# SAGE sums of a four-layer graph stack: h stored as three bf16 pieces

## The chip, the cores and the metric

The kernel runs on one core of a Trainium2 chip. The metric is device time in microseconds, from the first to the last instruction of the core. Before the change three runs gave 2575.82, 2585.0 and 2585.8 us; their median is 2585.0.

## The reference

There are 3327 nodes with 512 features (padded to 3328 rows, 26 blocks of 128) and a sparse 0/1 adjacency matrix. Four layers follow each other, each in the form x = x + layer(relu(layernorm(x))). Layers 0, 2 and 3 are graph attention with 8 heads. Layer 1, which the change is about, is GraphSAGE:

```python
mask = (adj > 0).astype(x.dtype)
deg = jnp.sum(mask, axis=1, keepdims=True)
agg = mask @ x / jnp.maximum(deg, 1.0)          # x here is h = relu(layernorm(x1))
self_f = x @ W_self + b_self
nb_f = agg @ W_nb + b_nb
out = jnp.concatenate([self_f, nb_f], axis=-1) @ W_comb + b_comb
return jax.nn.relu(out)
```

All of it is in float32.

## The kernel before, in words

**Neighbours by lists.** The rows of the output are taken in 52 groups of 64. For each group a first stage makes a list of the nodes that are a neighbour of any row in it, in chunks of 128. `CAPS` holds the number of chunks of each group: 22 for the first, down to 4 for the last, 359 in all. `mask` holds, for each chunk, a 128 x 64 matrix of 0 and 1 in one byte each. A chunk's 128 rows are fetched from a table in device memory by an indirect DMA that POOL issues (`gather`, L1115).

**Layer 0** ends with its output in `y`, 26 blocks of 128 x 512 float32 in on-chip memory. What comes next is the part that the change touches:

- Batch norm statistics: DVE, ACT and PE form the variance (L1352 to L1361).
- The norm stage. `normed(c)` works on two blocks. DVE applies batch norm and the residual (L1370 to L1372), the result goes to `x1`, DVE takes layer norm statistics (L1377), ACT makes h in place in `y` (L1385), and SP stores both blocks to `h_dram`, 512 float32 a row (L1386). `own(c)` then transposes a block of h, multiplies by the folded weights of the self half (PE, `s_ps`, L1396) and adds a bias into `y` (DVE, L1397). In program order `own` of a pair comes after `normed` of the next pair; all `normed` have their inputs at once, so DVE can run ahead of PE.
- SAGE. A block of 128 output rows is two groups, u = 0 and 1. `parts` cuts their chunks into units of up to `SUNIT` = 2 chunks. `load(i)` copies the masks of a unit to float32 on ACT (`z_mask`, L1453) and gathers up to two chunks of h (`z_rows`); `SROWS` = 8 units of buffers rotate, and the loads run `SAHEAD` = 2 parts ahead. Then PE adds mask.T @ rows into `sage_acc` (L1472): group u has the 64 output partitions from u * 64, so the two groups use different column halves of the array. Before each pair of chunks `tick()` moves on the work that follows: `ending` scales the finished sum by the degree, transposes it, multiplies by the folded neighbour weights (`n_ps`, L1421), adds and stores `x2`, and `proj` (an instance of `Following`) makes layer 2's table row by row (`p_ps` L795, `p_sd` L803, `p_wh` L816, `p_tr` L824).

No gather can start before the whole of `h_dram` is stored, since a list can name any row.

**Order and memory.** In the attention layers the order on PE, DVE and ACT is written out by hand. In the norm stage and SAGE it is not: the compiler orders ready instructions by program order and by its own estimate of times. Pools of on-chip memory are laid on each other as a stack. `proj = following(...)` at L1344 takes the memory of layer 2's projection, and starts its weight load `fWt` (1 MB, L749), before the batch norm stage.

Of the kernel before, what the change touches and what calls it, by code (L numbers as in the profile page):

```python
# [23 lines left out]
F32 = mybir.dt.float32  # L24
BF16 = mybir.dt.bfloat16
# [7 lines left out]
ALU = mybir.AluOpType  # L33
# [5 lines left out]
P = 128  # L39
H = 8  # L40
F = 64
D = H * F
# [8 lines left out]
GB = 64  # L51
CAPS = (22, 15, 13, 12, 11, 10, 9, 9, 9) + 4 * (8,) + 6 * (7,) + 11 * (6,) + 21 * (5,) + (4,)
# [5 lines left out]
UNIT = 3  # L58
SUNIT = 2
SROWS = 8  # L60
SAHEAD = 2
SMALL = 53.0
SHIFT = 20.0
# [638 lines left out]
def rsqrt(nc, pool, cs, v, scale=1.0, bufs=3):  # L702


    n = v.shape[1]
    y = pool.tile([P, n], F32, name="rs_y", tag=f"rs_y{n}", bufs=bufs)
    g = pool.tile([P, n], F32, name="rs_g", tag=f"rs_g{n}", bufs=bufs)
    nc.scalar.activation(g, v, AF.Ln, scale=scale, bias=cs["eps"])
    nc.scalar.activation(y, g, AF.Exp, scale=-0.5)

    def step():
        h = pool.tile([P, n], F32, name="rs_h", tag=f"rs_h{n}", bufs=bufs)
        nc.vector.tensor_scalar(h, v, -0.5 * scale, -0.5 * EPS, ALU.mult, ALU.add)
        if n == 1:
            nc.vector.tensor_scalar(g, y, y, h, ALU.mult, ALU.mult)
        else:
            nc.vector.tensor_tensor(g, y, y, ALU.mult)
            nc.vector.tensor_tensor(g, g, h, ALU.mult)
        nc.vector.scalar_tensor_tensor(y, g, 1.5, y, ALU.add, ALU.mult)
        return y  # L720

    return step
# [364 lines left out]
def sparse(ctx: ExitStack, tc: tile.TileContext, t: dict, out: bass.AP, WA, ls, cs, idx, rdeg, first):  # L1087
# [5 lines left out]
    nc = tc.nc  # L1093
    N = out.shape[0]
    NP = t["x"].shape[0]
    NB = NP // P
    NCH = ls.n
    PG = P // GB

    def used(c):  # L1100
        return min(P, N - c * P)

    dram = ctx.enter_context(tc.tile_pool(name="fdram", bufs=1, space=DRAM))
# [10 lines left out]
    def gather(dst, src, k):  # L1114
        nc.gpsimd.indirect_dma_start(  # L1115
            out=dst, out_offset=None, in_=src[:, :], in_offset=bass.IndirectOffsetOnAxis(ap=idx[:, k : k + 1], axis=0)
        )


    def attend(layer, table, r_dram, finish, tick=lambda: None, home=None):  # L1120
# [11 lines left out]
        with tc.tile_pool(name=f"fatt{layer}", bufs=2) as ap, tc.tile_pool(  # L1132
# [57 lines left out]
            def load(i):  # L1190
# [8 lines left out]
                if layer == 0:  # L1199
# [8 lines left out]
                    nc.scalar.activation(mask[:, k0 : k0 + n, :], on[:, :n].rearrange("p k w b -> p k (w b)"), AF.Sign)  # L1208

            load(0)  # L1210
            for i, (g, k0, n, begins, stops) in enumerate(units):
                gt = rows.pop(i)
# [9 lines left out]
                wt = ap.tile([P, UNIT, H, GB], F32, name="wgt", tag="wgt", bufs=3)  # L1222
                nc.vector.tensor_tensor(wt[:, :n], mx[:, :n], mk.unsqueeze(2).to_broadcast(full), ALU.mult)  # L1223
                load(i + 1)
                later()
                if begins:
# [22 lines left out]
    def following(lx, layer, wl, W, pb=1):  # L1249

        table = dram.tile([NP, ROW], I32, name=f"table{layer}")
        r_dram = dram.tile([ls.G, 2, H, GB], F32, name=f"r_dram{layer}")
        pp = lx.enter_context(tc.tile_pool(name=f"fproj{layer}", bufs=1))
        pps = lx.enter_context(tc.tile_pool(name=f"fproj_ps{layer}", bufs=1, space=PSUM))
        return Following(tc, cs, N, wl, W, WA, table, r_dram, pp, pps, pb)
# [20 lines left out]


    wx_dram = dram.tile([2, KC, P, D], F32, name="wx_dram")
    h_dram = dram.tile([NP, D], F32, name="h_dram")
    with ExitStack() as mx:  # L1280
        mid = mx.enter_context(tc.tile_pool(name="fmid", bufs=1))

# [58 lines left out]
        Wx = mid.tile([P, 2, KC, D], F32, name="fWx")  # L1341
        nc.sync.dma_start(Wx, wx_dram.rearrange("k kc p o -> p k kc o"))

        proj = following(mx, 2, 1, t["L2_gnn_W"], 2)  # L1344
        gp = mx.enter_context(tc.tile_pool(name="fsage", bufs=2))
        gps = mx.enter_context(tc.tile_pool(name="fsage_ps", bufs=2, space=PSUM))
        two = [P, 2, D]
        with tc.tile_pool(name="fbn", bufs=1) as bp:
            var_ps = gps.tile([P, D], F32, name="var_ps", tag="n_ps")
            for c in range(0, NB, 2):  # L1350
# [3 lines left out]
                for i in range(2):  # L1354
                    k = used(c + i)
# [7 lines left out]
        with tc.tile_pool(name="fln", bufs=1) as bp:  # L1363


            def normed(c):
                xr = bp.tile(two, F32, name="bn_x", tag="bn_x", bufs=3)
                nc.sync.dma_start(xr, t["x"][c * P : (c + 2) * P, :].rearrange("(k p) o -> p k o", p=P))
                yy = y[:, c : c + 2, :]
                nc.vector.tensor_tensor(yy, yy, gam.unsqueeze(1).to_broadcast(two), ALU.mult)  # L1370
                nc.vector.tensor_tensor(yy, yy, bet.unsqueeze(1).to_broadcast(two), ALU.add)
                nc.vector.scalar_tensor_tensor(xr, yy, 0.0, xr, ALU.max, ALU.add)  # L1372
                nc.sync.dma_start(x1[c * P : (c + 2) * P, :].rearrange("(k p) o -> p k o", p=P), xr)
                mv = bp.tile([P, 2, nc.vector.BN_AGGR_DIM], F32, name="ln_mv", tag="ln_mv", bufs=3)
                for i in range(2):
                    st = bp.tile([P, nc.vector.BN_STATS_DIM], F32, name="ln_st", tag="ln_st", bufs=3)
                    nc.vector.bn_stats(st, xr[:, i, :])  # L1377
                    nc.vector.bn_aggr(mv[:, i, :], st)
                r = rsqrt(nc, bp, cs, mv[:, :, 1:2].rearrange("p k o -> p (k o)"))()
                if c + 2 == NB:  # L1380
                    nc.vector.tensor_tensor(r[:, 1:2], r[:, 1:2], cs["real"], ALU.mult)
                ng = bp.tile([P, 2, 1], F32, name="ln_ng", tag="ln_ng", bufs=3)
                nc.vector.scalar_tensor_tensor(ng, mv[:, :, 0:1], -1.0, r.unsqueeze(2), ALU.mult, ALU.mult)
                for i in range(2):
                    nc.scalar.activation(yy[:, i, :], xr[:, i, :], AF.Relu, scale=r[:, i : i + 1], bias=ng[:, i, :])  # L1385
                nc.sync.dma_start(h_dram[c * P : (c + 2) * P, :].rearrange("(k p) o -> p k o", p=P), yy)  # L1386

            def own(c):
                tp = gps.tile([P, KC, P], F32, name="h_ps", tag="a_ps")
                for kc in range(KC):  # L1390
                    nc.tensor.transpose(tp[:, kc, :], y[:, c, kc * P : (kc + 1) * P], cs["ident"])
                hT = bp.tile([P, KC, P], F32, name="hT", tag="hT", bufs=2)
                nc.scalar.copy(hT, tp)  # L1393
                ps = gps.tile([P, D], F32, name="s_ps", tag="n_ps")
                for kc in range(KC):
                    nc.tensor.matmul(ps, hT[:, kc, :], Wx[:, 0, kc, :], start=(kc == 0), stop=(kc == KC - 1))  # L1396
                nc.vector.tensor_tensor(y[:, c, :], ps, bias, ALU.add)  # L1397

            for c in range(0, NB, 2):
                normed(c)  # L1400
                for i in range(2):
                    if c:
                        own(c - 2 + i)
            for i in range(2):
                own(NB - 2 + i)

        ends = []

        def ending(b, acc):
# [21 lines left out]
        def tick():  # L1431
            for e in list(ends):
                if next(e, 0) == 0:
                    ends.remove(e)
            proj.tick()
# [6 lines left out]
        loaded = {}  # L1442

        def load(i):
            if i >= len(parts):
                return
            zs = loaded[i] = []
            for u, kn in enumerate(parts[i][1]):
                if kn is not None:
                    k0, n = kn  # L1450
                    zt = gp.tile([P, SUNIT, D], F32, name="z_rows", tag="z_rows", bufs=SROWS)
                    mf = gp.tile([P, SUNIT, GB], F32, name="z_mask", tag="z_mask", bufs=SROWS)
                    nc.scalar.copy(mf[:, :n, :], mask[:, k0 : k0 + n, :])  # L1453
                    for k in range(n):
                        gather(zt[:, k, :], h_dram, k0 + k)
                        zs.append((k, u, k0 + k, mf[:, k, :], zt[:, k, :]))
            zs.sort(key=lambda x: x[:2])

        for i in range(SAHEAD):
            load(i)  # L1460
        for i, (b, _, begins, stops) in enumerate(parts):
            load(i + SAHEAD)
            if begins:
                acc = gps.tile([P, D], F32, name="sage_acc", tag="sage_acc")
            at = -1
            for r, u, k, m, z in loaded.pop(i):
                if r != at:
                    at = r
                    tick()
                g = b * PG + u  # L1470
                f, l = k == ls.first[g], k == ls.first[g] + CAPS[g] - 1
                nc.tensor.matmul(acc[u * GB : (u + 1) * GB, :], m, z, start=f, stop=l)  # L1472
            if stops:
                ends.append(ending(b, acc))
        while ends:
# [4 lines left out]
    with ExitStack() as l3:  # L1480
        at2 = proj
        proj = following(l3, 3, 2, t["L3_gnn_W"])
# [90 lines left out]
```

## Time and profile before

The profiled execution took 2951.92 us, with a span of 2950.1 us; the runs without the profiler have a median of 2585.0 us. All times of single instructions below are of the profiled execution.

| what | profiled execution |
|---|---|
| span | 2950.1 us, mean granted TensorE clock 0.791 |
| PE, DVE, ACT, POOL busy | 73%, 60%, 38%, 47% of the span |
| norm stage, first h_dram store to last | 954.7 to 1020.7 us |
| SAGE, first gather to last | 1024.6 to 1610.6 us |
| software DMA queue (all gathers) | 404.86 MB, 47.2% of 16 engines' span |
| all HBM reads and writes | 498.74 MB and 59.68 MB |

In a row of the profile, `z_rows<-h_dram,idx` means that the instruction writes `z_rows` and reads `h_dram` and `idx`; then come the number of instructions, the sum of their time and the mean of one in ns, and the idle time of the engine just before them with what ended it. PEld is PE's loading of weights, which can run beside a matmul. A busy share tells how full an engine is, not whether it sets the pace.

### The profile page before, as it was taken

The page shows a single profiled execution, that of the slowest core. Times are in us where ns is not written, and L with a number is a line of the kernel's source. Part 1 is how long each engine was busy: PE and PEld are TensorE (multiplying, and loading weights), DVE is VectorE, ACT ScalarE, POOL GpSimd, SP SyncE. Part 2 cuts the span into 40 slices and gives each one's busy share as a digit, 9 for nine tenths or more (in the row PEclk, how much of TensorE's full clock was granted, in tenths as well). Part 3 has the DMA queues.
Part 4 walks back from the last instruction along what each step waited for, and adds up shares of the span by engine and source line. Part 5 has one row for each costly group of instructions (what it writes and reads, how often), then busy time and mean ns, then how long its engine had stood idle before and what let it go on. Part 6 is the DMA issues. An engine that isn't in the chain of part 4 may idle for free.

```text
span 2950.1 us, 54237 instructions
## 1 busy us (share of the span) xinstructions
PE 2161.4 (73%) x21320; PEld 1372.2 (47%) x21320; DVE 1781.5 (60%) x2194; ACT 1115.7 (38%) x4044; POOL 1381.8 (47%) x1482
## 2 busy tenths in 40 slices
PE   4777577767775976888998567877777657767775
PEld 2444354555552422233333355655555345556564
DVE  7648587878786800011111377777776277888886
ACT  4543022333434412344455213555666501232333
POOL 1001365666550055665554365555444066666563
PEclk9778688977777997899999777777787766675765
DMA  7761577877662746666665466666565166667774
GB/s 309 282 251 46 174 235 233 252 214 209 201 203 82 246 145 187 189 207 212 198 196 183 133 184 186 200 198 188 178 178 166 45 192 190 193 200 198 201 205 131
DMA packets 188773, 562.09 MB, mean 191 GB/s; under 512 B 37732, under 2 KB 42272, under 8 KB 185182
## 3 DMA queue, kind: packets, MB, share of 16 engines
q0 software_dynamic: 115456, 404.86, 47.2%
q1 hardware_dynamic: 73054, 153.67, 14.7%
q8 instruction: 171, 2.80, 0.4%
q14 instruction: 92, 0.75, 0.1%
HBM read 498.74 MB, written 59.68 MB: 189 GB/s over the span
## 4 chain that ended last, share of the span: by engine, by line
PE 54%; issue 16%; ACT 9%; another core or an unknown queue 3%; DVE 3%; DMA 2%; POOL 1%; SPq 0%; DVEq 0%; ACTq 0%; POOLq 0%
PE facc L1237 28%; PE p_wh L816 7%; PE sage_acc L1472 5%; PE n_ps L1421 3%; PE r_bc L1148 2%; PE p_sd L803 2%; PE s_ps L1396 2%; ACT v_row L820 2%; ACT fhp L1175 1%; PE fwx_ps L1314 1%; PE bmean_ps L1324 1%; PE p_ps L795 1%; ACT hT L798 1%; DMA rows<-table,idx 1%
## 5 line engine op out<-in xcount | busy, mean ns | idle before, releaser
L1115 POOL DMA_INDIRECT rows<-table,idx x1077 | 1023.4, 950 | 873.2 <-PE facc L1237 361.7
L1237 PE MATMUL facc<-rows,wgt 128*64 128x65 f32 x17232 | 975.3, 268 | 412.7 <-issue 394.5
L1237 PEld LDWEIGHTS facc<-rows,wgt 128*64 128x64 f32 x17232 | 826.5, 176 | 628.7 <-issue 576.9
L1223 DVE TENSOR_TENSOR wgt<-mx,mask 128x1536 f32<-128x1536 f32 (+1 forms) x405 | 638.4, 1576 | 158.6 <-PE facc L1237 75.0
L1216 DVE TENSOR_TENSOR mx<-r_bc,rows 128x1536 f32<-128x1536 f32 (+1 forms) x405 | 639.6, 1579 | 144.7 <-PE facc L1237 65.9
L1115 POOL DMA_INDIRECT z_rows<-h_dram,idx x359 | 339.4, 945 | 387.0 <-ACT hT L1393 139.5
L1175 ACT ACTIVATE fhp<-sums,rd 64x64 f32<-64x64 f32 x832 | 219.8, 334 | 137.0 <-DVE rd L1169 71.8
L1472 PE MATMUL sage_acc<-z_rows,z_mask 128*64 128x512 f32 x718 | 225.2, 639 | 9.5 <-DMA z_rows<-h_dram,idx 6.2
L816 PE MATMUL p_wh<-fWt,hT 128*128 128x512 f32 x416 | 227.7, 695 | 1.4 <-ACT s_col L810 1.4
L1165 ACT COPY sums<-facc 128x260 f32<-128x260 f32 x156 | 57.7, 370 | 405.0 <-PE facc L1237 354.3
L813 DVE TENSOR_SCALAR s_col<-s_col 128x8 f32<-128x8 f32 x52 | 9.2, 177 | 306.0 <-issue 135.9
L1208 ACT ACTIVATE mask<-on 128x192 uint8<-128x192 uint16 (+1 forms) x135 | 46.5, 344 | 378.8 <-DVE on L1202 214.1
L816 PEld LDWEIGHTS p_wh<-fWt,hT 128*128 128x128 f32 x416 | 90.3, 228 | 109.8 <-issue 105.3
L820 ACT ACTIVATE v_row<-p_wh,v_row 128x64 f32<-128x64 f32 x416 | 90.4, 328 | 125.8 <-PE p_wh L816 99.3
L1426 DVE TENSOR_TENSOR s_o<-n_ps,bn_y 128x512 f32<-128x512 f32 x26 | 18.0, 691 | 192.2 <-issue 95.6
L1036 POOL DMA_DIRECT2D list_b<-shift x12 | 5.9, 503 | 273.4 <-DVE shift L990 273.4
L680 PE MATMUL wh_ps<-fWt,hT 128*128 128x512 f32 x208 | 128.9, 777 | 0.0
L803 PE MATMUL p_sd<-WA,hT 128*128 128x16 f32 x416 | 74.4, 303 | 70.3 <-ACT hT L798 46.2
L803 PEld LDWEIGHTS p_sd<-WA,hT 128*128 128x128 f32 x416 | 71.8, 246 | 103.9 <-ACT hT L798 59.6
L1175 ACT ACTIVATE bn_y<-sums,rd 64x64 f32<-64x64 f32 x416 | 109.5, 333 | 2.4 <-DVE rd L1169 0.5
L1421 PE MATMUL n_ps<-fWx,aT 128*128 128x512 f32 x208 | 106.1, 646 | 5.6 <-ACT aT L1417 5.5
L1148 PE MATMUL r_bc<-r_two,fones 2*128 2x512 f32 x156 | 95.3, 615 | 14.8 <-issue 8.1
(198 smaller groups left out, 2108.0 us busy)
## 6 DMA issues: line engine op xcount, KB each, us to landing
adj_i<-in_adj SPq DMA_DIRECT2D x26, 1664.0 KB
table<-v_row SPq DMA_DIRECT2D x78, 264.0 KB
rows<-table,idx POOLq DMA_INDIRECT x1077
fin_x<-fx SPq DMA_DIRECT2D x52, 256.0 KB
ln_x<-in_x SPq DMA_DIRECT2D x26, 256.0 KB
bn_x<-in_x SPq DMA_DIRECT2D x13, 512.0 KB
fx<-bn_x SPq DMA_DIRECT2D x13, 512.0 KB
fsage_x<-fx SPq DMA_DIRECT2D x26, 256.0 KB
```

The costliest lines, as they stand in the source:

```text
L680: nc.tensor.matmul(wh, hT[:, kc, :], self.Wt[:, kc, :], start=(kc == 0), stop=(kc == KC - 1))
L803: nc.tensor.matmul(sd[:, : 2 * H], hT[:, kc, :], WA[wl][:, kc, :], start=(kc == 0), stop=(kc == KC - 1))
L816: nc.tensor.matmul(wh, hT[:, kc, :], self.Wt[:, kc, :], start=(kc == 0), stop=(kc == KC - 1))
L820: nc.scalar.mul(V[:, h, 0:F], wh[:, h * F : (h + 1) * F], V[:, h, F : F + 1])
L1115: nc.gpsimd.indirect_dma_start(out=dst, out_offset=None, in_=src[:, :], in_offset=bass.IndirectOffsetOnAxis(ap=idx[:, k : k + 1], axis=0))
L1148: nc.tensor.matmul(rb, ones[0:2, :].bitcast(F32R), rrs.pop(g).bitcast(F32R), start=True, stop=True)
L1175: nc.scalar.mul(hp[o0 : o0 + GB, h * F : (h + 1) * F], sm[mine, q, 0:F], rd[mine, q, :])
L1216: nc.vector.tensor_tensor(mx[:, :n], rbs[g].unsqueeze(1).to_broadcast(full), gt[:, :n, H * (F + 1) : ROW].unsqueeze(3).to_broadcast(full), ...
L1223: nc.vector.tensor_tensor(wt[:, :n], mx[:, :n], mk.unsqueeze(2).to_broadcast(full), ALU.mult)
L1237: nc.tensor.matmul(accs[g][v * GB : (v + 1) * GB, q * (F + 1) : (q + 1) * (F + 1)], wt[:, k, h, :], gt[:, k, h * (F + 1) : (h + 1) * (F + 1)],
L1421: nc.tensor.matmul(ps, aT[:, kc, :], Wx[:, 1, kc, :], start=(kc == 0), stop=(kc == KC - 1))
L1472: nc.tensor.matmul(acc[u * GB : (u + 1) * GB, :], m, z, start=f, stop=l)
```

## The change

h is made as before, and then split into three bf16 numbers whose sum is h: the upper 16 bits of the float32 number (read in place, as every second 16-bit word), the upper 16 bits of what is left, and the rest. `h_dram` holds the three pieces side by side, 1536 bf16 numbers a row (3072 bytes in place of 2048). The mask is copied to bf16, and a chunk's sum is three matmuls with bf16 operands, one for each piece, all added into the same float32 accumulator. Within a part the loop now goes over chunk pairs, then pieces, then the two groups. The memory of the next layer's projection is allotted after the norm stage rather than before it, and its weight load moves with it.

```diff
+PIECES = 3
...
-    h_dram = dram.tile([NP, D], F32, name="h_dram")
+    h_dram = dram.tile([NP, PIECES * D], BF16, name="h_dram")
...
-        proj = following(mx, 2, 1, t["L2_gnn_W"], 2)
         gp = mx.enter_context(tc.tile_pool(name="fsage", bufs=2))
...
-                nc.sync.dma_start(h_dram[c * P : (c + 2) * P, :].rearrange("(k p) o -> p k o", p=P), yy)
+                for i in range(2):
+                    hi = yy[:, i, :].bitcast(BF16)[:, 1::2]
+                    hp = bp.tile([P, PIECES, D], BF16, name="h_pieces", tag="h_pieces", bufs=2)
+                    rest = bp.tile([P, D], F32, name="h_rest", tag="h_rest", bufs=2)
+                    nc.vector.tensor_tensor(rest, yy[:, i, :], hi, ALU.subtract)
+                    nc.scalar.copy(hp[:, 0, :], hi)
+                    hi = rest.bitcast(BF16)[:, 1::2]
+                    nc.vector.tensor_tensor(hp[:, 2, :], rest, hi, ALU.subtract)
+                    nc.scalar.copy(hp[:, 1, :], hi)
+                    b = c + i
+                    nc.sync.dma_start(h_dram[b * P : (b + 1) * P, :], hp.rearrange("p t o -> p (t o)"))
...
+        proj = following(mx, 2, 1, t["L2_gnn_W"], 2)
         ends = []
...
-                    zt = gp.tile([P, SUNIT, D], F32, name="z_rows", tag="z_rows", bufs=SROWS)
-                    mf = gp.tile([P, SUNIT, GB], F32, name="z_mask", tag="z_mask", bufs=SROWS)
+                    zt = gp.tile([P, SUNIT, PIECES * D], BF16, name="z_rows", tag="z_rows", bufs=SROWS)
+                    mf = gp.tile([P, SUNIT, GB], BF16, name="z_mask", tag="z_mask", bufs=SROWS)
...
-            at = -1
-            for r, u, k, m, z in loaded.pop(i):
-                if r != at:
-                    at = r
+            zs = loaded.pop(i)
+            for r in range(SUNIT):
+                now = [z for z in zs if z[0] == r]
+                if now:
                     tick()
-                g = b * PG + u
-                f, l = k == ls.first[g], k == ls.first[g] + CAPS[g] - 1
-                nc.tensor.matmul(acc[u * GB : (u + 1) * GB, :], m, z, start=f, stop=l)
+                for j in range(PIECES):
+                    for _, u, k, m, z in now:
+                        g = b * PG + u
+                        f = k == ls.first[g] and j == 0
+                        l = k == ls.first[g] + CAPS[g] - 1 and j == PIECES - 1
+                        nc.tensor.matmul(acc[u * GB : (u + 1) * GB, :], m, z[:, j * D : (j + 1) * D], start=f, stop=l)
```

## The prediction

> **What bounds the kernel now.** I read the page first for the costs and shapes, then windows of busy time to find what the change can reach, then the chain of waits and POOL's order of time inside them. The diff touches two neighbouring stages: the norm stage (942 to about 1020 us of the span, where h is made and stored) and SAGE (first gather at 1024.6, last PE sum at 1632 us). Elsewhere no instruction changes. From the windows of busy time (length, then busy us of PE, PEld, DVE, ACT and POOL with counts, granted clock, DMA share, GB/s):
>
> ```profile
> 942.00:1020.00 78.00, 63.21 (x186) 31.33 (x187) 76.17 (x173) 32.93 (x68) 0.00 (x0) 0.90 0.74 259
> 1046.00:1075.00 29.00, 27.91 (x80) 12.28 (x81) 4.15 (x6) 4.35 (x10) 5.66 (x7) 0.94 0.19 58
> 1075.00:1111.00 36.00, 19.91 (x60) 4.66 (x56) 0.00 (x0) 4.08 (x15) 27.41 (x29) 0.92 0.68 199
> 1300.00:1632.00 332.00, 297.74 (x994) 119.57 (x990) 41.34 (x128) 165.74 (x703) 180.15 (x191) 0.95 0.62 194
> ```
>
> The norm stage is DVE's: 76 of 78 us. From 1046 to 1075 PE is full (own halves of the rows) and the gathers stand. From 1075 to 1111 the gathers lead: 29 in 36 us, PE half idle. From 1300 on PE is 90% busy. So inside SAGE two limits alternate, POOL's stream of gathers and PE, and neither has much room. POOL's order of time shows both its pace and its stops:
>
> ```profile
> 1024.60 0.94 POOL L1115 DMA_INDIRECT z_rows<-h_dram,idx  x1 [139.47 <-ACT hT L1393]
> 1043.35 0.94 POOL L1115 DMA_INDIRECT z_rows<-h_dram,idx  x1 [0.30 <-issue]
> ...
> 1057.98 0.94 POOL L1115 DMA_INDIRECT z_rows<-h_dram,idx  x1 [8.30 <-PE sage_acc L1472]
> ...
> 1066.97 0.94 POOL L1115 DMA_INDIRECT z_rows<-h_dram,idx  x1 [6.79 <-PE sage_acc L1472]
> ...
> 1075.00 0.94 POOL L1115 DMA_INDIRECT z_rows<-h_dram,idx  x1 [5.84 <-PE sage_acc L1472]
> 1076.25 0.94 POOL L1115 DMA_INDIRECT z_rows<-h_dram,idx  x1 [0.30 <-issue]
> ```
>
> One gather each 1.25 us when nothing stops it (16 from 1024.60 to 1043.35), then stops while PE works off its own rows. All 359 cost 449 us at that pace; from 1024.6 to the last at 1610.6 it is 586, so POOL stands for 137 us. The waits of that stretch say for whom:
>
> ```profile
> POOL z_rows L1115 <- PE sage_acc L1472: 92.8, 34, 8.3
> POOL z_rows L1115 <- PE p_tr L824: 46.4, 10, 7.3
> POOL z_rows L1115 <- remote: 12.4, 4, 4.4
> ```
>
> The PE waits are slots that PE's sums have not freed. The sums themselves, from the page:
>
> ```profile
> L1472 PE MATMUL sage_acc<-z_rows,z_mask 128*64 128x512 f32 x718 | 225.2, 639 | 9.5 <-DMA z_rows<-h_dram,idx 6.2
> L1115 POOL DMA_INDIRECT z_rows<-h_dram,idx x359 | 339.4, 945 | 387.0 <-ACT hT L1393 139.5
> ```
>
> Two records for a chunk. In order of time 34 of them run from 1073.65 in 7.94 us, the two halves of 64 columns at once: (7.94 - 0.59 of the last one's length) / 17 = 0.43 us for a record, 0.86 for a step of one or two chunks. The chain of waits puts 12% of 1020 to 1660 us on "another core or an unknown queue"; such pieces are stalls of ACT. The longest starts in the first burst of gathers:
>
> ```profile
> 1032.79 13.59 another core or an unknown queue
> ```
>
> **What the Trainium skill says.** "FP8 and Floating Point Precision", TensorE Precision Notes: true fp32 takes four passes through the array. The trace agrees if each of the two records holds two passes; then a pass over 512 columns is 0.43/2 = 0.214 us. "TensorE: Matmul & The Clock Gate", Back-to-back issue gap, gives 216 ns for a bf16 matmul of 512 columns; no row here shows one, so 0.214 is an estimate from the records that this page supports. "VectorE: DVE Perf Modes", perf-mode tier table: tensor_tensor with fp32 operands has no faster mode; the trace's 128x512 fp32 bn_stats and sums at 0.60 us from start to start agree. "Runtime: NRT & Kernel Launch", Instruction fetch mechanics: instructions come by DMA in 16 KiB blocks, "mostly hidden". The page's instruction queue (171 packets, 2.80 MB) fits the size; the ACT stalls end when the gathers run dry (ACT resumes at 1046.45, DMA share 0.74 before 1046 and 0.11 after), so hidden is not what I see, if they are fetches at all.
>
> **The change, part by part.**
>
> The split, 26 blocks: two DVE subtractions and two ACT copies each. DVE: 52 x 0.60 us = 31 us (bounds 28, were a bf16 result somewhat quicker, and 36 at the full 0.69 us of such a row). DVE has 2 us of idle in this stage, so the norms end 31 us later; while they last, DVE also serves some 7 more of the additions after own (L1397) at 0.60 us, 4 to 5 us. ACT: 52 x 0.59 us (hT copy, 128x512) = 31 us onto 33 of the stage, hidden beside DVE. Two waits are new: DVE's first subtraction waits for ACT's relu, with the next pair's norm queued behind it on DVE (other pairs' work can stand before it, since all norms are ready), and the pieces, in two buffers, wait for the store of two blocks ago, some 3 us against 9 us for two blocks. The store grows from 6.8 to 10.2 MB, in 26 issues of 0.36 us rather than 13; DMA share 0.74 over 78 us becomes about 0.6 over 114, hidden. The last store, issued at 1020.7, moves to about 1057 and the first gather from 1024.6 to about 1061: +36.
>
> What that costs: PE needed until 1073.7 for own. With DVE at about 9 us a pair of blocks against PE's 8.25 (the spacing of 965.94, 974.19, 982.43), own still ends near 1065 to 1072. The stops of POOL at 1044 to 1075 (8.30 + 6.79 + 5.84 + 3.20 = 24 us) were lost time and go. So by 1075 the stream is behind by 36 - 24 = 12 us. Were own also pushed out, it is up to 20; were PE's stops longer than counted, 5.
>
> The sums: a step goes from four passes, 0.86 us, to three, 0.64: 0.21 saved. The caps in pairs make 186 steps; 55 of them lie in the first four blocks, which hold 101 of the gathers and run at the gathers' pace (1075 to about 1175), so nothing is won there. The other 131 give 28 us of PE. Weights are now loaded three times for a chunk rather than twice, 64 columns at 0.14 us, beside the passes of the other half; if they don't hide, a pass is nearer 0.27 and the saving is nil. A wait that PE no longer causes is worth its time only until the next gather is late, and a gather is due each 1.25 us: 258 x 1.25 = 323 of the 435 us left. I take half, 14 us; bounds 0 and 28.
>
> The gathers: a row grows from 2 to 3 KB, a gather from 262 to 393 KB, POOL's 945 ns for the same 128 indices stay. DMA time of one now: share 0.72 of 1.25 us in the first burst, 0.90 us. With half of it fixed per row it becomes 1.15, in proportion 1.35. I take 1.2 plus 0.08 us of the stage's other traffic, just above 1.25. About 275 of the 359 gathers follow their predecessor without a stop; 0.04 us each is 11 us; bounds 0 and 275 x 0.20 = 55.
>
> The stalls of ACT: they last until the gathers run dry, so with more bytes in the 16 gathers in flight some 0.3 us for each of about a dozen pieces, 4 us; bounds 0 and 25.
>
> The projection later: its 1 MB of weights, loaded at 899.96 us in an idle spot, is loaded after the norm pool is let go, near 1066, into the stretch where the gathers lead: 3.6 us at 290 GB/s (bounds 0 and 6). SP's queue has nothing urgent behind it: the first p_wh is at 1132. The mask copy to bf16 costs ACT what it did (289 ns). More instructions on PE (1,077 for 718, with as many loads) are inside the passes.
>
> Sum: 12 - 14 + 11 + 4 + 4 = +17 on a profiled execution of 2951.9 us (span 2950.1). The runs shown have a median of 2585.0, an eighth less, and the profile can't say where. Scaled by that eighth, +17 is +15: **2600 us**.
>
> **Rivals.**
>
> (a) PE decides to the end, and the change is faster. For it: 298 of 332 us busy after 1300. Then the 28 us come in full, the pace stays 1.25, and the stalls don't grow: 12 + 4 - 28 = -12, and if the later start is hidden too, 12 less, -24: 2564 to 2574. It decides as long as a gather, with its bytes, stays under 1.25 us. Against it: POOL's 137 us of slack shrink by the later start.
>
> (b) The DMA decides. For it: share 0.7 whenever the stream runs. At 1.35 + 0.1 us a gather the stream takes 0.2 us more for 275 gathers, nothing of PE's saving is seen: 12 + 55 + 10 + 4 = +81, less what POOL's stops for PE absorb, about half: 2620 to 2650. It decides from well over 1.25 us a gather on. Against it: the share of 0.7 holds only in the bursts; over 1300 to 1632 it is 0.62.
>
> (c) The passes don't come out at a third less (loads not hidden): 12 + 11 + 4 + 4 = +31, 2615. The change then doesn't do what it says. Against it: the loads of 0.14 us hide now beside passes of 0.21.
>
> **How the numbers follow.** The forecast's mechanism (later stream, half the saving, a slightly slower stream) has 0.45, (a) 0.2, (b) 0.2, (c) 0.15. The forecast's own range is 2585 to 2620. A measurement can tell about 0.5%, 13 us, from no change. Of the forecast 0.18 falls within that and the rest above; of (a) 0.16 below and 0.04 within; (b) and (c) are above but for 0.03. Faster 0.16, same 0.25, slower 0.59. Leaving out the ends of (a) and (b): 2565 to 2640.
>
> **What would show it.** After: DVE still full to about 1055 and h_dram's last store near 1057; first gather near 1061; sums in 1,077 records with 0.21 us from step to step in a full run; gathers of 1.25 us spacing with a DMA share near 0.95 in the first burst; POOL's waits on PE down from 139 us to under 90. A first gather before 1045, or a span from the first gather to the last of under 530 us, would make it wrong on the fast side; a spacing of 1.4 us or more on the slow one.

## The result, and the profile after

The changed kernel takes 2622.9 us (median of 4 runs, 2619.2 to 2627.3), the kernel before takes 2583.6 us (4 runs). The ratio is 1.0176, 95% interval 1.0157 to 1.0196: 39 us slower. The forecast was 15 us slower.

The kernel before takes near 2580 us in some sessions (runs made together) and 14 to 16% longer in others; the profile that the prediction was read from is of the longer kind (2951.9 us) and the profile after (span 2617.4 us) is not, so each run below is compared with the kernel before in the same session, whose time stands beside it.

The costliest groups of instructions of the changed kernel (busy us, mean ns, then idle time before them and what ended it):

```profile
L1116 POOL DMA_INDIRECT z_rows<-h_dram,idx x359 | 342.1, 953 | 339.8 <-ACT hT L1405 178.4
L1488 PE MATMUL sage_acc<-z_rows,z_mask 128*64 128x512 bf16 x1077 | 180.2, 422 | 21.2 <-DMA z_rows<-h_dram,idx 21.0
L1488 PEld LDWEIGHTS <-z_mask 128*64 128x64 bf16 x1077 | 62.6, 115 | 141.0 <-issue 109.7
L796 PE MATMUL p_ps<-fident,ln_h 128*128 128x128 f32 x208 | 42.3, 329 | 78.6 <-ACT ln_h L789 42.6
```

The sums are cheaper, as the change meant: 180 us of PE where they were 225, in 1,077 records. The last line is new as a cost (the kernel named move below has 2.8 us of this wait). PE stands for 42.6 us in front of `p_ps`, the transposes of layer 2's table that stand between SAGE's sums on PE, because ACT has not finished `ln_h`.

The norm stage is still DVE's, and longer (window of busy time from just before the first store to the last; length, then busy us of PE, PEld, DVE, ACT, POOL with counts, granted clock, DMA share, GB/s):

```profile
862.00:966.00 104.00, 96.35 (x284) 47.23 (x285) 100.77 (x210) 62.92 (x124) 0.00 (x0) 0.97 0.55 201
```

DVE has 101 of 104 us. POOL's order of time has the first gather right behind it, and then the even pace without the stops that the profile before had here:

```profile
969.72 0.95 POOL L1116 DMA_INDIRECT z_rows<-h_dram,idx  x1 [178.40 <-ACT hT L1405]
970.98 0.94 POOL L1116 DMA_INDIRECT z_rows<-h_dram,idx  x1 [0.31 <-issue]
972.22 0.95 POOL L1116 DMA_INDIRECT z_rows<-h_dram,idx  x1 [0.30 <-issue]
```

The windows of busy time inside SAGE show what comes after (same columns):

```profile
1000.00:1100.00 100.00, 76.83 (x318) 30.91 (x314) 6.78 (x19) 31.90 (x126) 75.64 (x81) 0.81 0.95 336
1100.00:1200.00 100.00, 81.49 (x331) 33.06 (x331) 9.23 (x28) 40.04 (x167) 63.62 (x68) 0.86 0.86 292
1200.00:1300.00 100.00, 89.76 (x353) 37.99 (x352) 11.77 (x35) 46.36 (x191) 61.78 (x65) 0.83 0.85 291
```

In the first 100 us POOL works 75.6 us, which is 80 gathers of 0.95 us or one per 1.25 us, its full pace, with a DMA share of 0.95. Then the gathers fall to 68 and 65, while PE isn't full either, its clock is at 0.83 to 0.86 and the DMA share falls too. No engine and no queue is full there; they wait for each other in turn. The waits between 1105 and 1300 us name the pair (us in total, times, longest):

```profile
POOL z_rows L1116 <- PE sage_acc L1488: 39.9, 24, 5.7
...
ACT z_mask L1466 <- PE sage_acc L1488: 32.2, 12, 5.0
PEld p_ps L796 <- ACT ln_h L789: 28.7, 8, 4.6
...
PE p_ps L796 <- ACT ln_h L789: 24.8, 8, 4.1
```

POOL and ACT wait for buffers that PE's sums free, and PE waits for ACT. One round of it in PE's order of time (start, length, instruction; in brackets the idle time before):

```profile
1143.90 1.98 PE L1434 MATMUL n_ps<-fWx,aT 128*128 128x512 f32 x4
1145.82 1.70 PE L1488 MATMUL sage_acc<-z_rows,z_mask 128*64 128x512 bf16 x13
1151.59 0.33 PE L796 MATMUL p_ps<-fident,ln_h 128*128 128x128 f32 x1 [4.07 <-ACT ln_h L789]
```

and in ACT's, between the same two instructions:

```profile
1147.38 0.63 ACT L778 ACTIVATE ln_j<-s_o 128x512 f32<-128x512 f32 x1 [3.07 <-DVE s_o L1440]
...
1150.72 0.81 ACT L789 ACTIVATE ln_h<-s_o,ln_s,rs_y 128x512 f32<-128x512 f32 x1
```

When `n_ps` ends at 1145.88, DVE adds, ACT and DVE take the layer norm, and `ln_h` is there at 1151.53: 5.7 us later. PE has 13 sums, 1.70 us, queued in that gap, and then stands 4.07 us, with all later sums behind it in PE's order. Of the 13 records twelve are pairs, the two halves at once, and the last stands alone: (1.70 - 0.38 of its length)/6 = 0.22 us from pair to pair, so a pass costs what was estimated (0.214).

### The profile page after: what moved, and what is told of

It reads as the page before. It is cut to its first block, busy times and chain, and to the rows that moved or that the text cites. A ratio compares the mean times of both kernels' runs of the same rounds, so it can differ in the third digit from the quotient of the medians.

```text
span 2617.4 us, 55116 instructions
## 1 busy us (share of the span) xinstructions
PE 1896.4 (72%) x21679; PEld 1250.7 (48%) x21679; DVE 1807.2 (69%) x2246; ACT 1142.0 (44%) x4096; POOL 1385.5 (53%) x1482
## 5 line engine op out<-in xcount | busy, mean ns | idle before, releaser
L1238 PE MATMUL facc<-rows,wgt 128*64 128x65 f32 x17232 | 765.6, 262 | 350.8 <-DVE wgt L1224 221.3
L1238 PEld LDWEIGHTS facc<-rows,wgt 128*64 128x64 f32 x17232 | 712.3, 175 | 473.3 <-DVE wgt L1224 270.4
L817 PE MATMUL p_wh<-fWt,hT 128*128 128x512 f32 x416 | 237.5, 712 | 1.4 <-ACT s_col L811 1.4
L1488 PE MATMUL sage_acc<-z_rows,z_mask 128*64 128x512 bf16 x1077 | 180.2, 422 | 21.2 <-DMA z_rows<-h_dram,idx 21.0
L1488 PEld LDWEIGHTS <-z_mask 128*64 128x64 bf16 x1077 | 62.6, 115 | 141.0 <-issue 109.7
L1408 PE MATMUL s_ps<-fWx,hT 128*128 128x512 f32 x208 | 94.2, 606 | 7.3 <-ACT hT L1405 7.3
L796 PE MATMUL p_ps<-fident,ln_h 128*128 128x128 f32 x208 | 42.3, 329 | 78.6 <-ACT ln_h L789 42.6
```

Source lines behind the costliest of these rows:

```text
L796: nc.tensor.transpose(tp[:, kc, :], hx[:, kc * P : (kc + 1) * P], self.cs["ident"])
L817: nc.tensor.matmul(wh, hT[:, kc, :], self.Wt[:, kc, :], start=(kc == 0), stop=(kc == KC - 1))
L1238: nc.tensor.matmul(accs[g][v * GB : (v + 1) * GB, q * (F + 1) : (q + 1) * (F + 1)], wt[:, k, h, :], gt[:, k, h * (F + 1) : (h + 1) * (F + 1)],
L1488: nc.tensor.matmul(acc[u * GB : (u + 1) * GB, :], m, z[:, j * D : (j + 1) * D], start=f, stop=l)
```

## The experiments

All kernels come from the kernel before or the changed one by the edit shown. Times are medians in us; +n is against the kernel before of the same session. Where start times are compared between kernels they are counted from the first variance matmul (`var_ps`) of the same execution, just ahead of the changed stages.

### The parts of the change, one at a time

Session with the kernel before at 2572.8.

**move**: only the projection's memory and weight load are allotted after the norm stage.

```diff
-        proj = following(mx, 2, 1, t["L2_gnn_W"], 2)
...
+        proj = following(mx, 2, 1, t["L2_gnn_W"], 2)
         ends = []
```

> The kernel before with the projection's memory and weight load moved, nothing else. Theory 1 (the later start of the gathers costs the 39 us) and theory 2 (the bytes of the 3 KB rows cost it) both expect 0 to +4 us against before. Theory 3 (the moved load and the new places in memory cost it) expects +15 us or more. Its profile is also the kernel before's order on an undisturbed execution: PE's sums in 718 records, gathers at 1.25 us, first gather near 1025 minus what the profiled execution of before lost.

Measured: 2571.7, ratio 0.9992 (0.9980 to 1.0005). The moved load costs nothing, and this kernel serves as the base of the others.

**split**: move, and the pieces are made and stored, but to a table that nobody reads; the sums still use float32 rows of 2 KB.

```diff
                 nc.sync.dma_start(h_dram[c * P : (c + 2) * P, :].rearrange("(k p) o -> p k o", p=P), yy)
+                for i in range(2):
+                    hi = yy[:, i, :].bitcast(BF16)[:, 1::2]
...
+                    nc.sync.dma_start(p_dram[b * P : (b + 1) * P, :], hp.rearrange("p t o -> p (t o)"))
```

> The move, and the split (two subtractions, two copies and a store of the pieces for each block) into a tensor that nobody reads; the sums stay fp32 on 2 KB rows. Theory 1: the first gather comes about 31 us later and most of it stays, +20 to +35 us against before. Theory 2: the later start is hidden by own's work, +0 to +12 us.

Measured: 2592.8, ratio 1.0069 (1.0046 to 1.0093), +20, the low end of theory 1.

**rows**: move, and rows of 3 KB (float32, the last third a copy that no sum reads; two stores for each block in place of one for two blocks).

```diff
-    h_dram = dram.tile([NP, D], F32, name="h_dram")
+    h_dram = dram.tile([NP, D + D // 2], F32, name="h_dram")
...
-                    zt = gp.tile([P, SUNIT, D], F32, name="z_rows", tag="z_rows", bufs=SROWS)
+                    zt = gp.tile([P, SUNIT, D + D // 2], F32, name="z_rows", tag="z_rows", bufs=SROWS)
```

> The move, and rows of 3 KB (h and half of it again) with the fp32 sums of before on the first 2 KB; no split. Theory 1: the gather stays at POOL's 1.25 us, 0 to +6 us against before. Theory 2: DMA share near 0.95 and a gather every 1.35 us or more while the gathers lead, +20 to +50 us.

Measured: 2620.9, ratio 1.0176 (1.0151 to 1.0201), +48: more than the whole change. The time is what theory 2 expected.

**passes**: move, and three bf16 passes on rows of 2 KB. The rows hold the upper half of h twice; the two lower pieces and the subtractions are left out, so a sum adds the upper half three times.

```diff
+                    nc.scalar.copy(hp[:, 0, :], hi)
+                    nc.scalar.copy(hp[:, 1, :], hi)
...
-                nc.tensor.matmul(acc[u * GB : (u + 1) * GB, :], m, z, start=f, stop=l)
+                for j in range(PIECES):
+                    for _, u, k, m, z in now:
...
+                        nc.tensor.matmul(acc[u * GB : (u + 1) * GB, :], m, z[:, j % 2 * D : (j % 2 + 1) * D], start=f, stop=l)
```

> The move, and three bf16 passes a chunk on rows of 2 KB that hold h's upper half twice (two ACT copies a block, no subtraction; two of the three pieces are left out, the second is read twice). If PE sets the pace of SAGE after the first blocks, -20 to -35 us against before; if the gathers do, -0 to -10 us; if loads of weights don't hide, 0. Steps of 0.64 us in a full run of sums.

Measured: 2562.1, ratio 0.9955 (0.9941 to 0.9970), -11. The two copies on ACT move its first gather from 119.6 us after `var_ps` in move to 128.2, so the passes alone may be worth somewhat more.

So the split and the passes give +20 - 11 = +9, if the two add up, and the puzzle is the 3 KB rows. In the trace of rows the gathers run at 1.25 us in the first burst, as in move; after the 100th they fall behind. So the spacing of 1.35 us or more, which theory 2 named, isn't there while the gathers lead. The two kernels, which differ only in the rows and their stores, have a different order of instructions on PE. Counted in chunks of sums that PE has before it (block 4 of 26 as the example):

```
kernel        n_ps       p_ps       p_wh
move          125        137        141
passes        122        138        138
rows          121-122    129-130    131-134
after         118-122    126-128    130-134
```

In the first ten blocks of move, `p_ps` stands 12 or more chunks behind `n_ps`; with 3 KB rows about 8 behind the first matmul of `n_ps` and 4 to 8 behind its last, and sums stand between the eight matmuls of one `n_ps` or `p_wh`. From the eleventh block on, move has 8 or 9 as well, and PE waits there only at the very end. Nothing in the text of the kernel asked for the difference. So two theories were left: the bytes cost the time themselves, or the order does that the compiler chose with them.

### One order for all

In the kernels named "fixed", SAGE's loop is put under a manual schedule, so that PE, DVE and ACT take the order of the program's text; there `p_ps` comes 8 chunks behind `n_ps`, and each product is unbroken.

```diff
+        with tc.manual_schedule(engines={ET.PE, ET.DVE, ET.Activation}):
             for i in range(SAHEAD):
                 load(i)
```

A fourth kernel, rows_passes, has 3 KB rows and three passes in the compiler's order, without the subtractions (the two lower pieces left out, the upper one three times).

> The move alone, with SAGE's order on PE, DVE and ACT fixed to the order of the program text (as the attention layers have it) rather than left to the compiler. It serves as the base for the next run. If the compiler's order is what suits 2 KB rows, +0 to +10 us against before; no theory of the 3 KB rows depends on it.

> 3 KB rows with the fp32 sums, in the same fixed order as the run before it, so that the two differ in bytes alone. Theory 2a (the bytes themselves: the queue is nearly full, rows land late, PE stands and its clock falls): +35 to +50 us against that base. Theory 2b (the compiler, reckoning with longer transfers, put PE's work in a worse order): +0 to +12 us.

> The changed kernel with the fixed order. Theory 2a: as the changed kernel, +30 to +45 us against before. Theory 2b: +0 to +20 us.

> 3 KB rows and three bf16 passes without the subtractions (two ACT copies of h's upper half, the second stored twice; two of the three pieces are left out). Theory 2: the bytes hide the passes' saving, within 8 us of the 3 KB rows with fp32 sums (+40 to +50 against before). If the passes' saving adds to it, +30 to +38. What is left to the changed kernel is the price of the split on top of these.

The kernel before took 2992.1 beside these four: move_fixed 2973.6 (0.9933, 0.9908 to 0.9958), rows_fixed 2982.6 (0.9962, 0.9946 to 0.9978), after_fixed 3005.4 (1.0046, 1.0033 to 1.0060), rows_passes 3011.9 (1.0061, 1.0035 to 1.0087). In the next session **two** was added: two pieces only, rows of 2 KB, two passes, one subtraction; the third piece of h is left out.

```diff
-PIECES = 3
+PIECES = 2
...
-                    rest = bp.tile([P, D], F32, name="h_rest", tag="h_rest", bufs=2)
-                    nc.vector.tensor_tensor(rest, yy[:, i, :], hi, ALU.subtract)
+                    nc.vector.tensor_tensor(hp[:, 1, :], yy[:, i, :], hi, ALU.subtract)
                     nc.scalar.copy(hp[:, 0, :], hi)
-                    hi = rest.bitcast(BF16)[:, 1::2]
-                    nc.vector.tensor_tensor(hp[:, 2, :], rest, hi, ALU.subtract)
-                    nc.scalar.copy(hp[:, 1, :], hi)
```

> The move with SAGE's order fixed, again, since all kernels of the last session, the one before included, took 15% longer with stalls put down to remote in all stages, and hid what was to be compared. Where those stalls are absent (before near 2575): 0 to +10 us against before. Where they are there (before near 2990): -10 to -30 us as in that session.

> 3 KB rows in that same order. Without the stalls, theory 2a (bytes): +35 to +50 us against the run before this; theory 2b (order): +0 to +12. With the stalls, +0 to +15 whatever the theory, since the gathers have slack while ACT stands.

> 3 KB rows and three passes without the subtractions (two of the three pieces left out), again for an execution without the stalls: theory 2, +40 to +50 us against before; if the passes' saving adds to the rows' cost, +30 to +38.

> h in two bf16 pieces (the third left out, so sums of about 16 bits): rows of 2 KB as before, two passes for four, one subtraction and one copy a block in the norm stage. If bytes were what cost the 39 us, it is not slower than before: the start of the gathers moves by some 16 us, of which 0 to 10 stay, and PE has up to 80 us less in sums, of which the gathers' own pace lets through 15 to 30: -10 to -30 us. If the split or the order were the cause, +5 to +20.

Beside these four the kernel before took 2949.1: move_fixed 2952.9 (1.0008, 0.9995 to 1.0022), rows_fixed 2944.0 (1.0000, 0.9979 to 1.0022), rows_passes 2977.3 (1.0084, 1.0055 to 1.0113), two 2953.7 (1.0008, 0.9992 to 1.0024). In both sessions rows_fixed loses nothing and rows_passes, in the compiler's order, loses 20 and 28 us. That hints at the order, but the two differ in the passes as well, and the 39 us were measured where the kernel before takes 2583.6. In a third session it took 2576.3:

> Base for the next run: the move with the order of the program text. Without the stalls 0 to +10 us against before, with them -20 to +5.

> 3 KB rows, same order. Without the stalls: bytes (2a) +35 to +50 us against the base; order (2b) 0 to +12. With the stalls: -5 to +10 in either case.

> The changed kernel in that order. Without the stalls: 2a +30 to +45 us against before, 2b 0 to +20. With the stalls +8 to +20, as before, from the later first gather.

> Two pieces in 2 KB rows, two passes (the third piece left out). Without the stalls: -10 to -30 us against before if bytes are the cause, +5 to +20 if split or order are. With the stalls 0 to +5, as before.

| kernel | median | ratio (95%) | +us |
|---|---|---|---|
| move_fixed | 2599.9 | 1.0080 (1.0054 to 1.0106) | +24 |
| rows_fixed | 2600.1 | 1.0092 (1.0075 to 1.0108) | +24 |
| after_fixed | 2632.6 | 1.0215 (1.0191 to 1.0240) | +56 |
| two | 2560.5 | 0.9931 (0.9914 to 0.9947) | -16 |

In one and the same order, rows of 2 and of 3 KB take the same time. The theory that the bytes cost the 48 us falls, as long as POOL's pace is what limits the gathers. (The -16 of two (two pieces) lies in the range set for the bytes, but two also has `p_ps` 9 to 16 chunks behind `n_ps` in the first ten blocks, so it can't tell the theories apart.) The windows of the fixed kernel with 3 KB rows show how near the two limits lie:

```profile
1054.80:1154.80 100.00, 92.66 (x315) 35.32 (x315) 9.81 (x30) 45.24 (x190) 75.77 (x80) 0.97 0.97 348
1154.80:1254.80 100.00, 89.72 (x342) 35.58 (x340) 13.25 (x41) 55.29 (x231) 75.62 (x79) 1.00 0.97 360
```

80 gathers in 100 us are POOL's 1.25 us, at a DMA share of 0.97. It just fits. The move alone shows that the order matters on its own too: the text's order costs move 24 us against the compiler's, where 0 to 10 had been expected. What the orders with `p_ps` at 8 chunks have in common is the wait. All of PE's waits for `ln_h` at `p_ps`, in the order move, fixed with 2 KB, fixed with 3 KB and rows in the compiler's order:

```profile
PE p_ps L795 <- ACT ln_h L788: 2.8, 1, 2.8
```

```profile
PE p_ps L795 <- ACT ln_h L788: 22.3, 18, 2.1
```

```profile
PE p_ps L795 <- ACT ln_h L788: 23.2, 19, 2.1
```

```profile
PE p_ps L795 <- ACT ln_h L788: 23.0, 13, 3.0
```

The +56 of after_fixed lies outside both theories. In its trace the wait is longer than in rows_fixed, in the same order with the same 8 chunks between, whose sums now take less time:

```profile
PE p_ps L796 <- ACT ln_h L789: 35.4, 23, 2.9
```

From SAGE's first sum to its last, PE is busy 430 us where it is 464 in rows_fixed, but idle 88 us where it is 49: the cheaper passes bring nothing there, and the later first gather (+34 us) stays in full.

That the place of `p_ps` does it was still only argued. The last two runs tried it.

### p_ps put back

In rows and in the changed kernel, the transposes are put two steps of the loop later (SAGE only) and tied behind the last sum traced. On PE they then come 12 chunks behind `n_ps` in block 4 (122 to 134) and 10 to 12 in nearly all blocks, more than move has in the later ones. What needs them (`p_sd`, `p_wh`, `p_tr`) comes later with them, and everything else is left to the compiler.

```diff
+        for _ in range(2 if hasattr(self, "after") else 0):
+            yield True
         tp = self.psum.tile([P, KC, P], F32, name="p_ps", tag="p_ps", bufs=self.pb)
-        for kc in range(KC):
-            nc.tensor.transpose(tp[:, kc, :], hx[:, kc * P : (kc + 1) * P], self.cs["ident"])
+        with behind(self.tc, self):
+            for kc in range(KC):
+                nc.tensor.transpose(tp[:, kc, :], hx[:, kc * P : (kc + 1) * P], self.cs["ident"])
...
-                        nc.tensor.matmul(acc[u * GB : (u + 1) * GB, :], m, z[:, j * D : (j + 1) * D], start=f, stop=l)
+                        proj.after = nc.tensor.matmul(acc[u * GB : (u + 1) * GB, :], m, z[:, j * D : (j + 1) * D], start=f, stop=l)
```

> rows (3 KB float32 rows, two-pass sums, projection moved) with the transposes p_ps of each block put two steps of the loop later and tied behind the last sum traced, so that on PE they come 12 chunks after n_ps, as in move, instead of 8. All else stays in the compiler's order. On executions without the long stalls (before near 2575): if the place of p_ps, where PE stood waiting for ln_h, is what rows lost its 48 us by, 0 to +20 against before; if the bytes did it, or some other part of the order, +40 to +50. If before takes near 2950 to 2990 this can't be told, and both say 0 to +10.

> the changed kernel with the same edit: p_ps 12 chunks after n_ps instead of 8. Without the long stalls (before near 2575): if the place of p_ps decides, the +39 falls to +10 to +22, what is left being the later first gather less what the cheaper passes give back; if it doesn't, +35 to +45. The waits of PE and PEld for ln_h (38.9 and 48.3 us in the changed kernel) should go in either case.

The kernel before took 2577.0 beside these two. rows_later: 2589.5, ratio 1.0049 (1.0034 to 1.0064), +12 where rows had +48. after_later: 2588.9, ratio 1.0053 (1.0035 to 1.0070), +12 where the change has +39. PE's wait for `ln_h` in after_later, and the windows of the same stretch as shown above:

```profile
PE p_ps L804 <- ACT ln_h L794: 1.4, 1, 1.4
```

```profile
1000.00:1100.00 100.00, 77.02 (x320) 31.20 (x319) 6.59 (x19) 31.35 (x122) 75.93 (x80) 0.79 0.94 330
1100.00:1200.00 100.00, 89.18 (x411) 39.78 (x412) 11.52 (x35) 51.22 (x215) 75.62 (x81) 0.91 0.98 355
1200.00:1300.00 100.00, 90.20 (x407) 38.42 (x406) 13.38 (x42) 55.48 (x229) 74.60 (x77) 0.98 0.97 350
```

The first window is the changed kernel's own. In the second and third POOL issues 81 and 77 gathers instead of 68 and 65, PE runs over 400 matmuls instead of some 340, and the clock is higher. Same bytes, same sums, same split: what was lost there hung on the place of four transposes per block and of the instructions behind them.

The wait itself is the smaller part of what was lost. The whole stretch from SAGE's first sum to its last, in the changed kernel and in after_later:

```profile
976.43:1486.31 509.88, 440.53 (x1882) 189.93 (x1881) 58.44 (x174) 238.96 (x991) 336.92 (x354) 0.88 0.89 314
```

```profile
975.44:1451.50 476.06, 417.87 (x1874) 179.63 (x1873) 56.48 (x169) 230.66 (x973) 338.05 (x354) 0.92 0.95 337
```

It is 34 us shorter. PE's idle time falls by 11 us only (69 to 58): the wait for `ln_h` goes, and that for gathered rows grows from 21.0 to 41.3 us. The other 23 us are PE's busy time. Eight matmuls of `p_wh` now come after the last sum, which is some 4 us; the rest are the same, and took less time at a granted clock of 0.92 in place of 0.88. The same holds for rows and rows_later: of 35 us, 11 are idle time and 24 busy time (ten matmuls fewer), at 0.95 and 0.99. What made the clock lower was not tried, so whether the waits did it isn't shown.

Not settled: rows and rows_fixed have the same wait at `p_ps` (23 us), and cost 48 and 24 us. So the wait is not the whole price of an order. Between SAGE's first and last sum PE is busy 507.7 us in rows and 463.9 in rows_fixed (third session), with 1,611 matmuls in both; why that is stays open. The broken-up products can't be much of the change's loss: in after_later sums still stand inside `n_ps` in 14 of 26 blocks (13 in the changed kernel), and it costs 12. Nor was it shown why the compiler orders otherwise with 3 KB rows. It sorts by its own estimate of times, and a longer gather is what differs; that is argued.

## Why the prediction was wrong, step by step

The sign held, and so did the outer range (2565 to 2640). The forecast's own range, 2585 to 2620, was missed by 3 us, and +15 was forecast where +39 was measured.

**The step that failed** is the sum 12 - 14 + 11 + 4 + 4. It prices what the diff touches and takes for granted that the instructions of SAGE which the diff doesn't touch keep their order. It has no term for the order of `p_ps`, `n_ps` and `p_wh` on PE, which is to put it at nothing without a reason, though the front of this text says that the compiler orders this stage by its own estimate of times. The missing term measures 39 - 12 = 27 us by the medians, and 2617.4 - 2584.7 = 33 us by the spans of the changed kernel and of after_later (where `p_ps` comes even later than in move from the eleventh block on). None of the rivals had it either. Outside the two stages "no instruction changes" held: from SAGE's last sum to the end it is 1131 us in the changed kernel and 1129 in move.

The terms that were in the sum (+12 - 14 + 11 + 4 + 4):

- *Later first gather, +36, of which 24 are regained.* The first gather came at 156.0 us after `var_ps` where move has 119.6: +36.4, as worked out. Regained were 17. Move takes 261.5 - 119.6 = 141.9 us from the first gather to 100 gathers later, which is 17 us of stops beyond 100 x 1.25; the changed kernel takes 281.0 - 156.0 = 125.0, no stops at all. So there it is 281.0 - 261.5 = 19.5 us behind, not 12. The 24 were read off the profile of 2951.9 us, where own's work on PE ends 168.6 us after `var_ps` (161.9 in move) and the stops were longer. Split alone ends with +20, as that says.
- *The sums, half of 28 saved, -14.* The pass came out at 0.22 us for 0.214, and the kernel with the passes alone gained 11, so taking only half was near. "TensorE: Matmul & The Clock Gate", Back-to-back issue gap, in the Trainium skill has 216 ns for the isolated gap of a 512-column matmul, and says that a sustained stream comes to about 131 ns for one; the prediction named the first alone. Here a pair of half-array matmuls, side by side, takes 0.22 us.
- *Gathers of 0.04 us more, +11.* Where the gathers lead, the pace stayed at 1.25 us with a DMA share of 0.94 to 0.98. In the fixed order the term is 0; in the compiler's, with `p_ps` put back, rows_later keeps +12, bytes or order. The share was foreseen (0.95).
- *ACT's stalls, +4.* The profile after has none of the waits "for a remote" at all, so there is nothing to lengthen, and the term was not tested.
- *The moved weights, +4.* Move: 0.

With the terms as measured, +20 - 11 and 0 to 12 for the rows, the sum is +9 to +21; after_later, which has the parts without the bad order, measures +12. So for the change without the bad order +17 was near, in part by luck: the first term was some 8 us too low and the last three too high, 19 us in place of 0 to 12. The compiled program had something else in it.

**Scaling.** +17 was brought to the runs by "an eighth less". What differs between the profile of 2951.9 us and the runs isn't a factor. By the first and the last gather, POOL had 137 us of slack in that profile, and in move, at 2570.4, 494.4 - 358 x 1.25 = 47 us. An edit that starts a stream later, or stops it, can be hidden in the first and show in the second: after_fixed costs 13 us (3005.4 - 2992.1) where the kernel before takes 2992.1, and 56 us where it takes 2576.3.

**The rivals.** (a), PE decides and the change gains, was wrong for the change, but passes and two show part of its mechanism: with 2 KB rows some of the sums' saving does arrive. (b), the DMA decides, gave 2620 to 2650, where the measured time lies, but by another mechanism: the spacing it needed, well over 1.25 us, isn't there in after_later or rows_fixed, with the same bytes. (c) was wrong, the passes came out a third less.

**The signs named ahead.** A DVE-bound split, the first gather +36, a share of 0.95 and 0.22 us per pass were all seen. One sign pointed the wrong way: a span from the first gather to the last of under 530 us was to mean a faster kernel, and the changed kernel, slower, has 502.6. The bound came from the 586 us of the profile before; move has 494.4. POOL's waits on PE were to fall below 90 us and did (62.8 for the sums and 11.5 for `p_tr`), which says little: in move they were 34.8 and 24.1 us, so against move they rose.

**A version that beats both.** Two pieces instead of three keep 2 KB rows: two, 2560.5, 0.9931 (0.9914 to 0.9947). It starts its gathers 18 us later than move (138.0 for 119.6) and starts SAGE's last sum 29 us earlier (599.9 for 629.4, both from `var_ps`); 12 of these are lost again after SAGE, which was not followed up. It keeps the upper 16 bits of h and a bf16 of what is left, so it is not the exact split that the change sets out to be.

## What to carry to other kernels

Where the compiler orders a stage, a change of a tile's size can reorder instructions that the diff doesn't touch: compare the order on the critical engine first, and then price the edit. Where PE takes the result of a long round trip through other engines, enough independent work has to stand ahead of it in PE's order to cover that trip (here 5.7 us against 1.7 us of sums); making the covering work cheaper shrinks the cover (23.2 us of waits in rows_fixed, 35.4 in after_fixed). Weigh such a wait by the whole stretch and not by its own length: here other waits took its place, and the clock moved. And before a profile is priced, see that its own time is that of the runs: slack read from an execution 14% longer wasn't there in the runs.

## What the runs showed of the hardware

- Waits for a remote. The profile before (2951.9 us) has 324.7 us in 147 of them, move_fixed and after_fixed beside the kernel before at 2992.1 have 391.9 and 367.7, move and the changed kernel none. Some lines of the profile before:

```profile
POOL rows L1115 <- remote: 79.4, 62, 3.7
...
ACT hT L798 <- remote: 43.6, 14, 4.9
```

  They sit on several engines. "Runtime: NRT & Kernel Launch", Instruction fetch mechanics, in the Trainium skill calls the cost of fetching the next block of instructions mostly hidden; whether these waits are fetches stays open.
- An indirect gather of 128 rows costs POOL the same with 2 and 3 KB a row (952 ns in move and 953 in the changed kernel, one per 1.25 us). With 3 KB and POOL at its full pace the DMA share is 0.97 and 348 to 360 GB/s are moved (rows_fixed, third session), so 3 KB is, by estimate from that share, about the longest row that this pace hides.
- The granted clock of TensorE was 0.83 from 1200 to 1300 us in the changed kernel, 0.98 in the same stretch of after_later. Between SAGE's first and last sum, PE's busy time times the clock is 440.5 x 0.88 = 388 us in the one and 417.9 x 0.92 = 384 us in the other, which has eight matmuls fewer there: the same matmuls took longer at the lower clock. Idle time of PE alone doesn't set that clock: in that stretch PE is idle for 53 of 524 us in move_fixed (third session) at 0.97, and for 37 of 545 us in rows at 0.95.
